# Attention over a convolved image: part sums added by accumulating transfers instead of VectorE

## The chip, the core and the metric

The kernel runs on one core of one Trainium2 chip. The metric is the device time of one execution in microseconds (us); less is better. Short names of the engines: PE is TensorE, DVE is VectorE, ACT is ScalarE, POOL is GpSimd, SP is SyncE. SP and POOL issue most of the transfers (DMAs).

## The reference

The input is four images of 384 channels and 48 x 48 points (2304 tokens). Of each image the reference computes

- `local`: a 7 x 7 convolution of each channel by itself, scaled and shifted, and a layer norm over the channels;
- `x_norm`: a layer norm of the image over the channels, and from it q, k, v by one 384 x 1152 product, in 8 heads of 48;
- `q = q + local`, `softmax(q k^T / sqrt(48)) v` for each head over all 2304 tokens, a 384 x 384 projection, and the sum of that and the image.

All of it is in 32-bit floats.

## The kernel before

**Tiling.** Channels lie on the partitions, tokens along the free axis. Two heads make a *pair*, so there are 4 pairs (`NP`). The queries of an image are worked in 5 *groups* (`NA`) of 8, 10, 10, 10 and 10 image rows, that is 384 or 480 tokens; with four images there are 20 groups, `t` = 0 to 19 (`NT`). The keys are 18 blocks of 128 (`KB`), taken in 3 batches of 6 (`BATCH`). A group therefore has 12 *slots* (`NSLOT`): slot `s` is pair `s // 3` and batch `s % 3`.

**A slot.** `score_batch` makes the scores of six key blocks on PE (L952), and ACT takes their exponentials (L960). `weigh_batch` multiplies them by the values on PE (L967) and sums over the six blocks in PSUM; the row behind the 48 of each head is the softmax's denominator, so the result of a pair stands on 64 + 49 = 113 partitions. `sums_out` then lets ACT copy it to SBUF. The first batch of a pair goes straight into the pair's place in `ao` (pairs 0 to 2) or `ao3` (pair 3, in the profile `aot`), by L859. The second and third go to a tile `part` of their own with tag `part_o` and two buffers (L849; in the profile the tile is `o`), and wait in the list `parts_of`. One `sums_add` in each slot takes the oldest of these and adds it to the pair's place (L868). After the third part it also issues, on SP, two small DMAs of the denominators to `den` in DRAM (L873), and after pair 3 six DMAs that bring rows of `ao3` to their place in `ao` (L877).

**The convolution.** Most of DVE's time goes to the convolution of the *next* group: 147 multiply-and-add instructions per group (L307), fed out of a queue `stream`. A planner (`plan`) deals them to points in the slots, from hand-estimated spare times; its numbers are fixed in the code. The next group's norm needs them done by a given slot: PE forms the mean over the channels (`mean_kept`, L568 with `mean_w`), DVE subtracts it (`centre`, L489), and so on to that group's queries (`query_end`, `high_queries`, `low_queries`). `low_queries` ends in SP DMAs that move rows inside the tile `qs` (L830, L832), and PE's scores wait for these.

**Between images** PE makes keys, values and queries of the next image in six steps (called the key stage here), and the output of the image before; DVE and ACT take their results from PSUM. Keys are written in pieces to `wide` in DRAM by POOL's DMAs (L591 to L619); in each slot one DMA (`load_keys`, L628) fetches the stack `ks` for two slots later, into one of three buffers.

**Division.** In slot 2 of the following group (or step 1 of the key stage) `divide` reads the denominators back, inverts them on DVE (L889), and spreads them by SP DMAs; in slot 7 DVE multiplies (L1259) and POOL stores the group's result (`hold`, L919).

**Order.** The instructions of PE, DVE and ACT stand in the order in which the program issues them. Those of POOL and SP are placed by a scheduler at build time, one queue each, and executed in that order: an instruction that waits holds up all behind it. POOL's DMAs also take turns on eight completion counters, so a DMA waits for an earlier one on its counter.

The first of the two places where a part is handed on:

```
        if i:
            part = work.tile([P, GM], F32, tag="part_o", name=f"o{t}_{p}_{i}")[:, :n]
            nc.scalar.copy(part[0 : 64 + HA], sums[0 : 64 + HA, 0, :n])
            parts_of.append((t, p, i, part))
            return
```

Of the kernel before, what the change touches and what calls it, by code (L numbers as in the profile page):

```python
# [13 lines left out]
ALU = mybir.AluOpType  # L14
# [33 lines left out]
def unshifted_pass(  # L48
# [16 lines left out]
    nc = tc.nc  # L65
# [10 lines left out]
    HA = HD + 1  # L76
    PAD = KS // 2
    NA = len(ROWS)
    NT = B * NA
# [121 lines left out]
    for c in range(CC):  # L201
        for r, n, first in ((0, HD, 0), (64, HD, 1), (48, 16, 6), (112, 16, 7)):
            head = first + 2 * c if first < 6 else first
            ch = head * HD + (16 * c if first >= 6 else 0)
            while n:
                part = min(n, P - ch % P)
# [654 lines left out]
    def sums_add():  # L861

        if not parts_of:
            return
        t, p, i, part = parts_of.popleft()
        ao, ao3, den = outputs[t]
        dst = (ao[:, p, :] if p < CC else ao3)[0 : 64 + HA]
        nc.vector.tensor_add(dst, dst, part[0 : 64 + HA])  # L868
        if i < KB // BATCH - 1:
            return  # L870
        for j in range(2):
            r = 64 * j
            nc.sync.dma_start(out=den[2 * p + j : 2 * p + j + 1], in_=dst[r + HD : r + HA])  # L873
        if p == NP - 1:
            for c in range(CC):
                for r in (0, 64):
                    nc.sync.dma_start(  # L877
                        out=ao[r + HD : r + 64, c, :], in_=ao3[r + 16 * c : r + 16 * c + 16]
                    )
# [231 lines left out]
    for t in range(NT):  # L1111
        b, g = divmod(t, NA)
        if g == 0 and b:

            sums_add()
            load_x(b, NG - 1)
            norms_x = {}
# [67 lines left out]
        for s in range(NSLOT):  # L1185
            pair, part = divmod(s, KB // BATCH)
# [40 lines left out]
            if early and s == first + 3:  # L1227
                low_queries(t + 1, 0)
            convolve("slot", t, s, 0)
            sums_add()  # L1230
            if early and s == first + 1:
                norm.centre()
# [39 lines left out]
            if following and s == first + 1:  # L1272
                norm.sum_squares()
                norm.out()

    sums_add()
    for i, at in enumerate(pieces_out):
        ao, n = aos[i], size(at)
# [555 lines left out]
```

## Time and profile before

| | |
|---|---|
| median of 3 runs | 2784.97 us (2781.41 to 2786.35) |
| the profiled execution: time / span of its trace | 2782.53 us / 2780.7 us |
| PE busy | 2749.9 us, 99% of the span |
| DVE busy | 2339.9 us, 84% |
| ACT busy | 1639.0 us, 59% |
| POOL busy | 696.2 us, 25% |
| mean share of the 16 DMA engines on POOL's queue / SP's queue | 35.4% / 12.2% |

The span runs from the first to the last instruction; the execution's time is 1.8 us longer. The shares of busy time are over all stages. A wait is written as the instruction that waited, and what released it. A line "L868" is that line of the kernel. In an entry such as `113x480 f32` the first number counts partitions, the second elements on each.

### The profile page before, as it was taken

What the parts mean: (1) busy time and instruction counts of PE and PEld (TensorE: products, weight loads), DVE (VectorE), ACT (ScalarE), POOL (GpSimd) and SP (SyncE); (2) the same over time, 40 slices, a digit from 0 to 9 for tenths busy, and PEclk for the clock granted to TensorE, in tenths of its full rate; (3) what the DMA queues carried; (4) which work ended last, traced back from release to release, by engine and by line L of the source; (5) the groups of instructions that cost most, each with busy time, mean ns of one, the idle gap of its engine ahead of it and who ended that gap; (6) DMA issues with size and microseconds to landing.
All of it is one profiled execution on the core that took longest, in us unless ns stands there. A gap on an engine that the chain in (4) does not pass through costs nothing.

```text
span 2780.7 us, 46399 instructions
## 1 busy us (share of the span) xinstructions
PE 2749.9 (99%) x16438; PEld 1555.9 (56%) x16438; DVE 2339.9 (84%) x4082; ACT 1639.0 (59%) x2281; POOL 696.2 (25%) x1273
## 2 busy tenths in 40 slices
PE   9998999999999999999999999999999999999999
PEld 6565555555555655555556665555555565555555
DVE  6879999989999999989888899898898889987112
ACT  4345666666423766776632566767652276676662
POOL 5731111111375111110257311101117701110110
PEclk9999999999999999999999999999999999999999
DMA  7344444445355454454545554545535545444442
GB/s 143 98 112 126 118 122 131 122 129 134 124 165 153 129 141 138 120 143 133 159 107 152 159 135 128 137 124 145 137 116 165 140 130 133 138 128 135 141 145 74
DMA packets 163298, 369.15 MB, mean 133 GB/s; under 512 B 61488, under 2 KB 112208, under 8 KB 163056
## 3 DMA queue, kind: packets, MB, share of 16 engines
q0 software_dynamic: 76992, 284.75, 35.4%
q1 hardware_dynamic: 83072, 77.72, 12.2%
q10 hardware_dynamic: 2992, 3.62, 0.4%
q8 instruction: 132, 2.16, 0.3%
q14 instruction: 110, 0.90, 0.1%
HBM read 258.14 MB, written 64.14 MB: 116 GB/s over the span
## 4 chain that ended last, share of the span: by engine, by line
PE 87%; DVE 5%; POOL 4%; DMA 2%; issue 1%; ACT 1%; SPq 0%; DVEq 0%; ACTq 0%; POOLq 0%
PE o L967 40%; PE r L952 32%; PE r L568 14%; DVE acc L307 4%; POOL wide L594 1%; DMA wide<-k 1%; DMA slab<-in_x_dram 1%; POOL wide L619 1%; POOL wide L592 1%; POOL wide L591 0%; POOL wide L613 0%; DVE k L661 0%; PE r L322 0%; DMA qs<-qs 0%; PE r L1010 0%
## 5 line engine op out<-in xcount | busy, mean ns | idle before, releaser
L307 DVE SCALAR_TENSOR_TENSOR acc<-slab,vec,acc 128x450 f32<-128x450 f32 (+8 forms) x2854 | 1679.8, 657 | 2.2
L960 ACT ACTIVATE pt<-r 128x960 f32<-128x960 f32 (+1 forms) x1440 | 1248.4, 943 | 236.4 <-PE o L967 148.9
L967 PE MATMUL o<-pt,v 128*64 128x480 f32 (+1 forms) x5760 | 1167.9, 555 | 4.1 <-ACT pt L960 4.1
L952 PE MATMUL r<-qs,ks 64*128 64x480 f32 (+1 forms) x8640 | 970.9, 374 | 9.5 <-DMA qs<-qs 6.3
L952 PEld LDWEIGHTS r<-qs,ks 64*128 64x128 f32 x8640 | 784.9, 184 | 277.6 <-issue 168.2
L967 PEld LDWEIGHTS o<-pt,v 128*64 128x64 f32 x5760 | 393.1, 137 | 663.7 <-issue 581.7
L628 POOL DMA_DIRECT2D ks<-wide x228 | 165.5, 726 | 1361.2 <-PE r L952 1328.9
L568 PE MATMUL r<-xn,w_qk 128*128 128x384 f32 x864 | 283.7, 486 | 0.0
L849 ACT COPY o<-o 113x480 f32<-113x480 f32 (+1 forms) x160 | 87.1, 544 | 299.4 <-PE o L967 299.4
L568 PEld LDWEIGHTS r<-xn,w_qk 128*128 128x128 f32 x864 | 164.2, 190 | 114.5
L868 DVE TENSOR_TENSOR ao<-ao,o 113x480 f32<-113x480 f32 (+1 forms) x120 | 76.1, 634 | 96.1 <-ACT o L849 96.0
L568 PE MATMUL r<-w_v,xn 128*128 128x384 f32 x432 | 144.8, 487 | 0.0
L650 ACT COPY v<-r 128x384 f32<-128x384 f32 x72 | 32.1, 480 | 188.3 <-PE r L568 188.3
L568 PEld LDWEIGHTS r<-w_v,xn 128*128 128x128 f32 x432 | 81.5, 190 | 58.3 <-issue 2.9
L594 POOL DMA_DIRECT2D wide<-k x192 | 96.6, 508 | 11.3 <-issue 8.3
L859 ACT COPY ao<-o 113x480 f32<-113x480 f32 (+1 forms) x60 | 32.7, 545 | 101.9 <-PE o L967 101.9
L619 POOL DMA_DIRECT2D wide<-k x192 | 92.7, 488 | 0.0
L613 POOL DMA_DIRECT2D wide<-k x144 | 72.1, 503 | 76.0 <-ACT k L658 60.4
L108 POOL DMA_DIRECT2D slab<-in_x_dram x76 | 47.1, 627 | 153.6 <-DVE acc L307 153.4
L825 DVE TENSOR_TENSOR qs<-xn,qs 128x480 fp32r<-128x480 f32 (+1 forms) x60 | 38.0, 633 | 56.2 <-ACT qs L820 56.1
L568 PE MATMUL r<-af,w_o 128*128 128x384 f32 (+1 forms) x270 | 85.2, 470 | 0.0
L675 ACT ACTIVATE xn<-r,qkb 128x384 f32<-128x384 f32 x72 | 41.0, 578 | 64.7 <-PE r L568 63.1
(139 smaller groups left out, 1348.1 us busy)
## 6 DMA issues: line engine op xcount, KB each, us to landing
ks<-wide POOLq DMA_DIRECT2D x228, 768.0 KB, 5.2
qs<-qs SPq DMA_DIRECT2D x352, 60.0 KB
wide<-k POOLq DMA_DIRECT2D x480, 24.0 KB, 1.9
slab<-in_x_dram POOLq DMA_DIRECT2D x24, 432.0 KB, 8.1
wide<-k POOLq DMA_DIRECT2D x192, 48.0 KB, 1.8
wide<-ks POOLq DMA_DIRECT2D x12, 768.0 KB, 4.4
xr<-in_x_dram POOLq DMA_DIRECT2D x16, 576.0 KB, 5.3
rb<-rden SPq DMA_DIRECT2D x32, 270.0 KB
```

The costliest lines, as they stand in the source:

```text
L108: queue.dma_start(out=dst[p0 : p0 + piece.shape[0]], in_=piece)
L307: nc.vector.scalar_tensor_tensor(dst, src, weight, dst, ALU.mult, ALU.add)
L568: nc.tensor.matmul(dst, lhsT=weights(c), rhs=src(c), start=c == 0, stop=c == CC - 1)
L594: queue.dma_start(out=dst[r + 32 * i : r + 32 * i + 32, 1], in_=k[r + 16 : r + HD, 1])
L613: nc.gpsimd.dma_start(out=last[16 * u : 16 * u + 16, 0], in_=k[r : r + 16, 0])
L619: nc.gpsimd.dma_start(out=last[to : to + 16, 1], in_=k[r : r + 16, 1])
L628: nc.gpsimd.dma_start(out=place_keys(b, p, i), in_=wide[b, p][:, :, at])
L849: nc.scalar.copy(part[0 : 64 + HA], sums[0 : 64 + HA, 0, :n])
L868: nc.vector.tensor_add(dst, dst, part[0 : 64 + HA])
L952: nc.tensor.matmul(r[:, j, :n], lhsT=ks[rows, w, at], rhs=qs[rows, m, :], start=i == 0, stop=i == 2,)
L960: nc.scalar.activation(pt, r[:, :, :n], AF.Exp, scale=SCALE)
L967: nc.tensor.matmul(sums[halves[j], 0, : columns_of(t)], lhsT=values[t // NA, kb // NB][:, first : first + 64], rhs=pt[:, j, :], start=i == ...
```

## The change

`sums_add` adds the second and the third part of a pair by a DMA on POOL's queue that reads the part and adds it to the destination in SBUF, instead of by a DVE instruction. In the last two groups the DVE instruction stays.

```
@@ -865,7 +865,10 @@
         t, p, i, part = parts_of.popleft()
         ao, ao3, den = outputs[t]
         dst = (ao[:, p, :] if p < CC else ao3)[0 : 64 + HA]
-        nc.vector.tensor_add(dst, dst, part[0 : 64 + HA])
+        if t < NT - 2:
+            nc.gpsimd.dma_start(out=dst, in_=part[0 : 64 + HA], accum_op=ALU.add)
+        else:
+            nc.vector.tensor_add(dst, dst, part[0 : 64 + HA])
         if i < KB // BATCH - 1:
             return
         for j in range(2):
```

Lines behind it move down by three (L952 becomes L955, and so on); the transfers stand at L869, the remaining instructions at L871. The order on DVE and ACT is otherwise the same. On POOL each transfer stands, by the build, between the key loads of its slots; on SP a few DMAs change places, among them, in the key stage, the read of the denominators (L888), which moves behind eight DMAs of the first key stack.

## The prediction

> **What bounds the kernel.** I read the page's busy times and chain first, then PE's waits, then the stretch where the longest of them lies, and last the transfers that are nearest to the new one.
>
> ```profile
> PE 2749.9 (99%) x16438; PEld 1555.9 (56%) x16438; DVE 2339.9 (84%) x4082; ACT 1639.0 (59%) x2281; POOL 696.2 (25%) x1273
> ...
> PE 87%; DVE 5%; POOL 4%; DMA 2%; issue 1%; ACT 1%; SPq 0%; DVEq 0%; ACTq 0%; POOLq 0%
> ...
> L868 DVE TENSOR_TENSOR ao<-ao,o 113x480 f32<-113x480 f32 (+1 forms) x120 | 76.1, 634 | 96.1 <-ACT o L849 96.0
> ```
>
> PE is the bound: 2780.7 - 2749.9 leaves it 30.8 us of idle time. The adds take DVE's time, and DVE even waits before them, but only what shortens PE's idle time can shorten the run. PE's own waits:
>
> ```profile
> PE r L568 <- DVE acc L307: 7.8, 1, 7.8
> PE r L952 <- DMA qs<-qs: 6.3, 5, 2.4
> PE o L967 <- ACT pt L960: 4.1, 3, 2.1
> PE r L952 <- ACT pt L960: 3.2, 4, 1.1
> ```
>
> (total, times, longest). Only the first waits for DVE: once, 7.8 us, for the convolution. It is in group 0, whose slots are the short ones (384 tokens). PE in order of time there (start, length, line, count, and in brackets the idle time before):
>
> ```profile
> 246.69 5.14 PE L568 MATMUL r<-acc,mean_w 128*128 128x480 f32 x6 [7.80 <-DVE acc L307]
> 251.76 3.48 PE L952 MATMUL r<-qs,ks 64*128 64x384 f32 x36
> 255.17 4.09 PE L967 MATMUL o<-pt,v 128*64 128x384 f32 x24
> 259.19 2.68 PE L568 MATMUL r<-sq,mean_w 128*128 128x480 f32 x6
> ```
>
> Six matmuls took 5.14 us after the wait, and six of the same form 2.68 us later. The table of stretches shows why (stretch, its length, busy time of PE, PEld, DVE, ACT and POOL, and then the granted clock, the DMA share and GB/s):
>
> ```profile
> 242.00:244.00 2.00, 0.00 (x0) 0.00 (x0) 1.89 (x4) 0.00 (x0) 0.00 (x0) 0.50 0.00 0
> ...
> 248.00:250.00 2.00, 2.00 (x3) 0.67 (x2) 2.00 (x4) 0.00 (x0) 1.90 (x4) 0.50 0.98 206
> ...
> 252.00:254.00 2.00, 2.00 (x24) 2.00 (x26) 2.00 (x4) 1.68 (x3) 0.00 (x0) 1.00 0.98 154
> ```
>
> In the wait the clock fell to half, and it came back only at about 252. So this place costs 7.8 us, and 2.5 us of slow matmuls.
>
> **What the change removes.** 18 groups of 8 adds: 144 of the 160. Of these 32 are in the groups of 384 tokens (rows of 0.55 us) and 112 in those of 480 (0.65 us): 32 x 0.55 + 112 x 0.65 = 90 us of DVE's 2339.9. Nearly all of it lies beside PE, which did not wait for DVE. On PE's path stand only the adds between the start of group 0's slots and the end of that convolution. DVE in order of time:
>
> ```profile
> 188.23 0.55 DVE L868 TENSOR_TENSOR ao<-ao,o 113x384 f32<-113x384 f32 x1
> 188.70 9.34 DVE L307 SCALAR_TENSOR_TENSOR acc<-slab,vec,acc 128x480 f32<-128x480 f32 x15
> 197.95 0.56 DVE L868 TENSOR_TENSOR ao<-ao,o 113x384 f32<-113x384 f32 x1
> ...
> 216.01 0.56 DVE L868 TENSOR_TENSOR ao<-ao,o 113x384 f32<-113x384 f32 x1
> ...
> 225.15 0.55 DVE L868 TENSOR_TENSOR ao<-ao,o 113x384 f32<-113x384 f32 x1
> ...
> 237.03 9.51 DVE L307 SCALAR_TENSOR_TENSOR acc<-slab,vec,acc 128x480 f32<-128x480 f32 x13
> 246.46 0.55 DVE L868 TENSOR_TENSOR ao<-ao,o 113x384 f32<-113x384 f32 x1
> ```
>
> Four adds stand before the convolution's end; the fifth begins as it ends. Each puts the next instruction back by 0.47 us (188.70 - 188.23), so the convolution ends 4 x 0.47 = 1.9 us sooner. No other work fills in, as DVE shows no wait here. The wait becomes 5.9 us; the clock had fallen after some 3 us of it, so the slow matmuls stay, and the gain is **1.9 us**, up to 2.5 if the clock returns a step sooner. What is late next is the 2.41 us wait for `qs` at 278: it hangs on ACT, on DVE's query instructions and on SP, has no add in front of it after 253, and stays. The key stages lose nothing: their waits (1.41 and 1.57 us in the first) hang on SP's queue of DMAs behind DVE's last keys, and the one add at their start (736.70, after 3.00 us of DVE waiting) is followed by other DVE waits of some 10 us in the same stage.
>
> The Trainium skill (TensorE: Matmul & The Clock Gate, Part 1) says that the clock halves after an idle window of about 3.4 us and that the window runs freely. By it a wait of 5.9 us still halves the clock, and the return can shift by a window from run to run.
>
> **What it adds on POOL.** 144 issues at 0.5 (a 48-row DMA) to 0.73 us (a key load) are 72 to 105 us on an engine that is idle for 1328.9 us before its key loads alone: hidden. Each transfer waits for ACT's copy, and the third part's also for the second part's landing, since both add to the same bytes. Behind a waiting transfer stand the next key load, slab and image loads; for its landing wait ACT's copy two parts later (two buffers), SP's `den` DMAs with the `qs` DMAs behind them, and then `divide`.
>
> **How long one takes** no row shows, since none accumulates. The nearest are:
>
> ```profile
> ks<-wide POOLq DMA_DIRECT2D x228, 768.0 KB, 5.2
> ...
> wide<-k POOLq DMA_DIRECT2D x480, 24.0 KB, 1.9
> ...
> held<-ao POOLq DMA_DIRECT2D x12, 720.0 KB, 3.8
> ```
>
> (count, KB each, us from issue to landing.) `held<-ao` moves 384 rows of 1920 B, `wide<-k` 16 rows. If both use all 16 DMA engines, they have 24 rows and 1 row on each, so a row costs (3.8 - 1.9) / 23 = 0.083 us. The new transfer has 113 rows of 1920 B: 8 on an engine, 1.9 + 7 x 0.083 = **2.5 us**; if reading the destination doubles the row, 3.1. But 113 is not a multiple of 16, as every row count above is. Should all rows go to one engine, it is 1.9 + 112 x 0.083 = 11.2 us, and doubled 20.5. I take 2.5 to 3.1: these DMAs are of the same kind on the same queue. The ends for the range are 2.5 and 20.5; below 2.5 nothing more would be gained, as the wait is not PE's.
>
> The Trainium skill (DMA: Bandwidth & Descriptors, "Why a DMA increments its semaphore by 16 and not by 1") speaks against my choice: the number of engines is the largest divisor up to 16 of the slowest dimension, which for 113 is 1, and only some direct copies on this queue are spread regardless. By it the sum would be that of the first rival below. No trace here shows such a row count.
>
> **What covers a landing.** A slot of 480 tokens is 9.08 us. After the second part's copy, POOL issues: that transfer, a key load, (9 us later) the third part's, a key load. The latter's keys are first read 4 x 9.08 = 36.3 us after the second part's PE work ends; copy 0.56 and issue 0.73 come off: 35.0 left for two landings, one after the other, and 5.2 of the load behind them: 2 x 3.1 + 5.2 = 11.4, or 9.08 + 3.1 + 5.2 = 17.4 with the slot between. Covered by far. ACT's copy needs its buffer 27 us after the transfer may start: covered. In a group's start, `den` waited for an add 4 us after ACT's copy (512.4 to 516.3); 0.7 + 3.1 is the same, so `divide` in slot 2 finds its numbers. In the key stage the read of the denominators moves from 742 behind the key stack, to about 755; DVE wants it at 765.74.
>
> **Sum.** 2782.5 - 1.9 = 2780.6 for an execution like the profiled one. The median is 2.4 above that execution, so the forecast is 2784.97 - 1.9 = **2783 us**: no change that a measurement can tell, whose bound I take at 0.2% or 5.6 us.
>
> **Rivals.**
> *One engine does all rows* (slower). The third part's transfer stands in that engine's queue before the key load's rows. It decides where 2 x L + 5.2 passes 35.0, at a landing L of 14.9 us. At 11.2 nothing is lost; at 16, 2.2 us for each of 72 pairs, 158 us; at 20.5, 11.2 x 72 = 806 us. For it: 113 rows, a read of the destination that no row here has. Against: POOL's loads of 16 and 48 rows land in about 2 us. Chance 0.20.
> *Crowding* (slower). In 210 to 220 us the DMA engines are 0.79 busy and PE already waits 0.44 us for `qs`; at 278 it waits 2.41. If a new transfer delays these two by 3.1 us each and the second wait also halves the clock (2.5 us), that is 8.7 - 1.9 = 6.8 more, 2792; with the same in the key stages' three starts, 3 x (3.1 + 2.5) = 17 more, 2809. Against: `qs` elsewhere has some 10 us to spare (issued 525.5, read from 539). Chance 0.15.
> *The wait vanishes* (faster). If DVE's convolution also ran quicker without the adds, by 5 us over the 66 us, the clock would hold, and 7.8 + 2.5 = 10.3 us would go: 2775. Against: the convolution's instructions have no wait behind an add. With the spread of 5 us between runs, chance 0.10.
> *Nothing of it reaches PE* gives 2785 and lies in the forecast, whose chance is 0.55.
>
> The forecast's own range is 2780 to 2788. For 8 in 10 the range takes in the third rival's half, all of crowding, and the foot of the first: 2777 to 2835; the rest of the one-engine case, about 0.15, is left out, and 0.03 below.
>
> **What would show it.** Right: no L868 adds before group 18, the wait at 246 near 5.9 us, the new transfers landing in 2.5 to 4 us, no new PE wait. Wrong: PE or ACT waiting for `ks`, or ACT's `o` copies waiting for a DMA; landings over 15 us; POOL's key loads released by a DMA and not by PE; or PE's waits at `qs` grown to several us.

## The result, and the profile after

The changed kernel takes **2795.22 us** (median of 7 runs, 2791.45 to 2798.54) where the kernel before takes 2784.97: ratio 1.0036, 95% interval 1.0026 to 1.0046. The forecast was 2783 us and no change that can be measured; it is 10 us slower, beyond the 5.6 us taken as the bound. The profiled execution took 2795.22 us, its span 2793.4 us against 2780.7, that is 12.7 us more.

The page's busy times, the chain, and the costliest groups' line of the new transfers (busy us, mean ns; idle time of POOL before them):

```profile
PE 2754.3 (99%) x16438; PEld 1561.1 (56%) x16438; DVE 2258.9 (81%) x3938; ACT 1638.7 (59%) x2281; POOL 828.9 (30%) x1417
...
PE 85%; DMA 5%; DVE 4%; POOL 3%; issue 2%; ACT 1%; SPq 0%; DVEq 0%; ACTq 0%; POOLq 0%
...
L869 POOL DMA_DIRECT2D ao<-o x108 | 97.9, 907 | 378.4 <-ACT o L849 303.2
```

DVE lost 81 us of work and POOL gained 133 us. PE is still the bound; its idle time went from 30.8 to 39.1 us and its busy time up by 4.4 us, though it executes the same matmuls. PE's waits (total, times, longest) say where the idle time came from:

```profile
PE r L955 <- DMA qs<-qs: 16.3, 10, 5.4
PE r L568 <- DVE acc L307: 6.0, 1, 6.0
PE o L970 <- ACT pt L963: 3.9, 3, 2.1
PE r L955 <- ACT pt L963: 3.2, 4, 1.0
```

The wait for the convolution shrank by 1.8 us, as forecast. The wait for `qs` grew by 10.0 us, from five places to ten. With the 4.4 us of slower matmuls that is 10.0 + 4.4 - 1.8 = 12.6 of the 12.7 us. In PE's timeline (start, length, line, count; idle time before and its end in brackets) the first line is the place in group 0, and the other four are waits that were not there before:

```profile
245.91 5.14 PE L568 MATMUL r<-acc,mean_w 128*128 128x480 f32 x6 [5.96 <-DVE acc L307]
...
996.57 4.17 PE L955 MATMUL r<-qs,ks 64*128 64x480 f32 x35 [1.26 <-DMA qs<-qs]
...
1110.87 6.39 PE L955 MATMUL r<-qs,ks 64*128 64x480 f32 x36 [5.37 <-DMA qs<-qs]
...
1673.78 3.69 PE L955 MATMUL r<-qs,ks 64*128 64x480 f32 x31 [0.55 <-DMA qs<-qs]
...
2030.52 5.08 PE L955 MATMUL r<-qs,ks 64*128 64x480 f32 x31 [2.35 <-DMA qs<-qs]
```

The longest shows the mechanism. ACT copied the part of pair 3 to `o`, and was done at 1078.90:

```profile
1078.34 0.56 ACT L849 COPY o<-o 113x480 f32<-113x480 f32 x1 [2.13 <-PE o L970]
```

POOL then did this:

```profile
1089.04 1.15 POOL L108 DMA_DIRECT2D slab<-in_x_dram  x1 [14.68 <-DVE acc L307]
1090.18 0.94 POOL L869 DMA_DIRECT2D aot<-o  x1
1090.76 1.52 POOL L108 DMA_DIRECT2D slab<-in_x_dram  x2
```

and SP this:

```profile
1095.08 0.50 SPq L876 DMA_DIRECT2D den<-aot  x2
1095.63 3.80 SPq L880 DMA_DIRECT2D ao<-aot  x6
1101.78 0.35 SPq L891 DMA_DIRECT2D rd<-den  x1
1102.23 0.51 SPq L832 DMA_DIRECT2D qs<-qs  x1
...
1105.68 1.32 SPq L832 DMA_DIRECT2D qs<-qs  x2
```

The first and the last of these in the kernel before:

```profile
1082.87 0.51 SPq L873 DMA_DIRECT2D den<-aot  x2
...
1093.15 1.34 SPq L832 DMA_DIRECT2D qs<-qs  x2
```

The transfer was ready to go at 1078.90 and was issued at 1090.18, 11.3 us later: ahead of it on POOL stood the image load of the next convolution (`load_slab`, L108), which waited 14.68 us until DVE's convolution let go of the buffer. SP's `den` DMAs came at 1095.08 instead of 1082.87 in the kernel before, and the last `qs` DMA, behind them on SP, was issued by 1107.0 instead of 1094.5. (Some 1.4 us of these 12 us are an earlier lag of the whole run: PE's scores of the slot before began at 1096.36 and 1095.00.) PE was ready for that pair at 1105.5 and waited 5.37 us. The table of stretches (PE busy, then the other engines; granted clock, DMA share, GB/s at the end) shows the second half of the price:

```profile
1106.00:1108.00 2.00, 0.00 (x0) 0.00 (x0) 0.00 (x0) 0.10 (x1) 0.00 (x0) 1.00 0.96 190
1108.00:1110.00 2.00, 0.00 (x0) 0.00 (x0) 0.00 (x0) 0.00 (x0) 0.88 (x1) 0.62 0.39 86
1110.00:1112.00 2.00, 1.13 (x5) 1.06 (x7) 1.89 (x6) 0.00 (x0) 0.00 (x0) 0.50 0.85 113
...
1114.00:1116.00 2.00, 2.00 (x14) 1.82 (x14) 2.00 (x4) 1.71 (x2) 0.00 (x0) 0.67 1.05 211
1116.00:1118.00 2.00, 2.00 (x15) 1.09 (x13) 1.90 (x5) 1.09 (x2) 0.45 (x1) 1.00 0.82 129
```

The clock fell to half in the wait and stayed there until about 1115, so the 36 score matmuls took 6.39 us where 4.15 were enough at 1096.

The wait of 1.26 us at 997 came in the same way: 8.3 us on POOL's queue, from the end of ACT's copy (968.21) to the issue (976.48). The other two new waits are of a second kind. Before the one of 2.35 us at 2030, POOL and SP did this:

```profile
2002.84 0.71 POOL L108 DMA_DIRECT2D slab<-in_x_dram  x1 [10.03 <-DVE acc L307]
2003.54 0.73 POOL L628 DMA_DIRECT2D ks<-wide  x1
2004.27 0.94 POOL L869 DMA_DIRECT2D ao<-o  x1
```

```profile
2014.99 0.52 SPq L876 DMA_DIRECT2D den<-ao  x2
```

The part was copied by 2000.69, so the queue held the transfer for only 3.6 us; but it took 10.7 us to land, where the median of all transfers is 4.0 (3.5 to 12.1), and SP's `den` DMAs, with `qs` behind them, waited for that. For the wait of 0.55 us at 1674 it was 4.4 us of queue and a landing of 11.6 us, from 1642.70 to 1654.3. The third part's transfer adds to the same bytes and had to wait for it: its part was copied by 1645.71, and it was issued at 1654.91. Both slow transfers were issued right behind DMAs of the image load and a key load of 768 KB; the transfer at 1090.18, with a single DMA of the image load just ahead of it, landed in 4.9 us. So a place behind the image load can cost twice, on POOL and in the landing. That the loads just ahead make the landing long is read from these three places and not tested by itself.

### The profile page after: what moved, and what is told of

It reads as the page before. It is cut to its first block, busy times and chain, and to the rows that moved or that the text cites. A ratio compares the mean times of both kernels' runs of the same rounds, so it can differ in the third digit from the quotient of the medians.

```text
span 2793.4 us, 46587 instructions
## 1 busy us (share of the span) xinstructions
PE 2754.3 (99%) x16438; PEld 1561.1 (56%) x16438; DVE 2258.9 (81%) x3938; ACT 1638.7 (59%) x2281; POOL 828.9 (30%) x1417
## 3 DMA queue, kind: packets, MB, share of 16 engines
q1 hardware_dynamic: 83072, 77.72, 12.1%
## 4 chain that ended last, share of the span: by engine, by line
PE 85%; DMA 5%; DVE 4%; POOL 3%; issue 2%; ACT 1%; SPq 0%; DVEq 0%; ACTq 0%; POOLq 0%
PE o L970 38%; PE r L955 31%; PE r L568 15%; DVE acc L307 2%; DMA qs<-qs 2%; DMA aot<-o 1%; DMA wide<-k 1%; DMA slab<-in_x_dram 1%; DMA ao<-aot 1%; POOL wide L594 1%; PE r L322 1%; POOL wide L619 1%; POOL wide L592 0%; POOL wide L591 0%; POOL wide L613 0%
## 5 line engine op out<-in xcount | busy, mean ns | idle before, releaser
L955 PE MATMUL r<-qs,ks 64*128 64x480 f32 (+1 forms) x8640 | 976.2, 375 | 19.4 <-DMA qs<-qs 16.3
L955 PEld LDWEIGHTS r<-qs,ks 64*128 64x128 f32 x8640 | 790.1, 185 | 287.7 <-issue 179.7
L628 POOL DMA_DIRECT2D ks<-wide x228 | 171.9, 754 | 759.0 <-PE r L955 659.5
L869 POOL DMA_DIRECT2D ao<-o x108 | 97.9, 907 | 378.4 <-ACT o L849 303.2
L825 DVE TENSOR_TENSOR qs<-xn,qs 128x480 fp32r<-128x480 f32 (+1 forms) x60 | 38.0, 633 | 98.2 <-ACT qs L820 98.1
L108 POOL DMA_DIRECT2D slab<-in_x_dram x76 | 51.9, 732 | 142.0 <-DVE acc L307 140.9
L460 DVE TENSOR_TENSOR sq<-sq 128x384 f32<-128x384 f32 (+1 forms) x33 | 19.5, 591 | 78.0 <-ACT sq L455 78.0
```

The lines of the kernel that those rows point to most:

```text
L108: queue.dma_start(out=dst[p0 : p0 + piece.shape[0]], in_=piece)
L628: nc.gpsimd.dma_start(out=place_keys(b, p, i), in_=wide[b, p][:, :, at])
L869: nc.gpsimd.dma_start(out=dst, in_=part[0 : 64 + HA], accum_op=ALU.add)
L955: nc.tensor.matmul(r[:, j, :n], lhsT=ks[rows, w, at], rhs=qs[rows, m, :], start=i == 0, stop=i == 2,)
```

## The experiments

Two theories stood at the start. **Q**, the queue: a transfer that stands behind a waiting image load on POOL starts some 10 us late, and its lateness goes through SP's queue to `qs` and PE. **C**, crowding: the transfers load the DMA engines, and everything on them, the `qs` DMAs among it, lands later. "Before" below is 2784.15 to 2784.80 us, run beside each set.

**Only pairs 0 to 2.** SP's chain of `den`, `ao<-aot` and `rd` hangs on pair 3, so the first pair of experiments splits the transfers there: 108 of the 144, then the other 36.

```
-        if t < NT - 2:
+        if t < NT - 2 and p < NP - 1:
```

> 108 transfers stay (pairs 0 to 2); the 36 sums of pair 3, behind which the denominators' DMAs of the whole group stand, go back to VectorE. Theory Q (queue): the loss comes from the transfers of pair 3 that stand on POOL's queue behind a slab load which waits for VectorE's convolution; SP's denominator and row DMAs wait for them, and the qs DMAs behind these come late. Then the PE waits at 997 (1.3 us), 1111 (5.4) and 1674 (0.6) vanish with their half clock, the one at 2030 (2.4, a pair below 3) may stay: ratio 1.000 to 1.001, 2784 to 2787 us. Theory C (crowding): the loss comes from the transfers' load on the DMA engines: three quarters of it stay, ratio 1.0027, about 2792 us.

Measured: 2785.17 us, ratio 1.0006 [0.9997, 1.0015]. Three quarters of the transfers cost nothing that can be measured. Of the four new waits one is left (2.51 us, at 2024), and one of 1.89 us is new at 1352. Both are of the second kind: these transfers were issued at 1997.58 and 1325.39 among the DMAs of an image load, and `den` followed 10.6 and 11.2 us later.

**Only pair 3.**

```
-        if t < NT - 2:
+        if t < NT - 2 and p == NP - 1:
```

> The reverse: only the 36 sums of pair 3 (18 groups) go by transfer, the 108 of pairs 0 to 2 by VectorE. Theory Q: the waits after group changes stay, ratio 1.002 to 1.004, 2790 to 2796 us. Theory C: a quarter of the load, ratio 1.001, about 2787 us.

Measured: 2800.38 us, ratio 1.0059 [1.0045, 1.0072]. A quarter of the transfers costs more than all of them, 4 us above the expected range. PE's longest wait for `qs` lies at the same place:

```profile
1118.80 6.43 PE L955 MATMUL r<-qs,ks 64*128 64x480 f32 x36 [4.80 <-DMA qs<-qs]
```

Its span is 6.1 us longer than that of the changed kernel. In three places PE waits 5.8 us more: the wait in group 0 (7.95 instead of 5.96, the VectorE adds are back there), the wait for `qs` in group 0 behind it (4.14 instead of 2.42), and the first scores of the second image (three waits of 2.77, 0.59 and 0.33 instead of one of 1.55). Elsewhere it waits less: its idle time grew by 4.1 us in all (43.2 instead of 39.1) and its busy time by 2.0. Why the latter two places grew was not followed up.

**All transfers, ahead of the image load.** POOL's queue is ordered at build time. Here the image load of the next group is told to stand behind the last transfer recorded, and the line that records the transfer moves ahead of the convolution's in the slot. The number of transfers and what they move stay.

```
     def conv_ops(t):
         if t + 1 < NT:
-            load_slab(*divmod(t + 1, NA))
+            with tc.issue_after(transfers[-1].ins) if transfers else ExitStack():
+                load_slab(*divmod(t + 1, NA))
...
-            convolve("slot", t, s, 0)
             sums_add()
+            convolve("slot", t, s, 0)
```

> All 144 transfers, but each sum is handed on ahead of the slot's convolution, and each slab load is queued on POOL behind the latest transfer, so that (but for one place in the third image) no ready transfer stands behind a slab load. Theory Q: the new PE waits vanish, ratio 0.999 to 1.001, 2782 to 2787 us. Theory C: the same bytes at nearly the same times, ratio 1.003 to 1.004, 2793 to 2797 us.

Measured: **2781.99 us**, ratio 0.9991 [0.9982, 1.0000]. The whole loss is gone. POOL's timeline of the same stretch, and PE's waits:

```profile
1080.23 0.86 POOL L873 DMA_DIRECT2D aot<-o  x1 [4.84 <-ACT o L852]
1089.82 2.27 POOL L108 DMA_DIRECT2D slab<-in_x_dram  x3 [8.72 <-DVE acc L310]
```

```profile
PE r L960 <- DMA qs<-qs: 7.3, 6, 2.5
PE r L571 <- DVE acc L310: 6.9, 1, 6.9
```

The transfer goes at 1080, right after ACT's copy, and the load, behind it, goes at 1089.82, where it went at 1089.72 in the kernel before. Crowding as the cause of the loss is refuted: 144 transfers with the same bytes on the same engines, and the wait for `qs` is 7.3 us where 6.3 was before. Single transfers still land late (3.5 to 12.3 us, median 3.9), but PE's six waits for `qs` all lie in group 0 and at the starts of images.

**Copy instead of accumulate**, at the same places. The kernel then leaves out the sums: the place of a pair holds only the last part.

```
-            nc.gpsimd.dma_start(out=dst, in_=part[0 : 64 + HA], accum_op=ALU.add)
+            nc.gpsimd.dma_start(out=dst, in_=part[0 : 64 + HA])
```

> The transfers copy the part over the sum and don't add it (the output lacks the other parts); order and waits are the same. What the addition costs by itself: landing 2.5 us (worked out from the plain rows) against 3.5 to 4.6. Theory Q: the transfers still stand behind the slab loads, ratio 1.002 to 1.0035. Theory C: the load of the added bytes halves or better, ratio below 1.0015.

Measured: 2792.32 us, ratio 1.0031 [1.0022, 1.0041]. The loss needs no accumulation; a plain copy at the same place in the queue costs nearly the same (7.9 us, where the changed kernel loses 10.3). What accumulating costs on the DMA engines is seen in the DMA issues (count, KB each, median us from issue to landing), first the changed kernel, then this one:

```profile
ao<-o POOLq DMA_DIRECT2D x84, 211.9 KB, 4.6
aot<-o POOLq DMA_DIRECT2D x28, 211.9 KB, 3.8
```

```profile
ao<-o POOLq DMA_DIRECT2D x84, 211.9 KB, 3.6
aot<-o POOLq DMA_DIRECT2D x28, 211.9 KB, 2.7
```

About 1 us more to land, and 0.91 instead of 0.56 us to issue on POOL.

**The denominators' DMAs behind `qs` on SP.** This cuts the way over SP inside an image, and leaves the transfers as late as they are.

```
+        late.append((t, p, dst))
+        if not (p == NP - 1 and t < NT - 2 and t % NA < NA - 1):
+            denominators()              # the den and ao<-aot DMAs
...
-                low_queries(t, pair + 1)
+                denominators(low_queries(t, pair + 1))   # issued after the last qs DMA
```

> All 144 transfers as in the changed kernel, behind the slab loads too; but within an image the DMAs that need pair 3's sums on SP (two den, six ao<-aot, and the read of the denominators behind them) stand behind the six qs DMAs of the next pair, not ahead of them. Theory Q (the late transfer reaches PE through SP's queue, where qs stands behind den): PE's waits at qs fall from 16.3 us to some 6, the two new ones of 1110 and 2030 are gone, and the time is 2782 to 2786. DVE still waits 40 us or more at the denominators, since the transfers are as late as before. Rival D (it reaches PE through DVE, whose reciprocal waits up to 15.7 us with the work of later slots behind it): the reciprocal comes even later, so the time stays at 2795 or goes above.

Measured: 2821.10 us, ratio 1.0134 [1.0118, 1.0149]: a miss, on the side of rival D. The trace holds both. The waits near 996, 1111 and 1673 are gone, as theory Q says. The one near 2030 is gone too, but not by this edit, which leaves the `den` DMAs of pairs 0 to 2 ahead of `qs`: in this run the transfer there was issued before the image load (2020.90 and 2029.67). The denominators are read later, though, and DVE's reciprocal, in order ahead of the later slots' work, now waits 133 us in 16 places instead of 46.5 us in 6:

```profile
DVE rd L909 <- DMA rd<-den: 133.1, 16, 16.4
```

```profile
1126.82 0.34 DVE L909 RECIPROCAL rd<-rd 128x30 f32<-128x30 f32 x1 [16.39 <-DMA rd<-den]
...
1147.03 0.65 DVE L825 TENSOR_TENSOR qs<-xn,qs 128x480 fp32r<-128x480 f32 x1
```

```profile
1154.98 1.17 PE L972 MATMUL r<-qs,ks 64*128 64x480 f32 x4 [4.29 <-DMA qs<-qs]
```

The query instruction of the pair after (L825) came so late that PE waited for that pair's `qs` instead. So a late transfer has two ways to PE: over SP, and over DVE. The edit closed one and widened the other.

**Transfers in group 0 alone**, the prediction's gain by itself (`if t == 0:`).

> Transfers in group 0 alone (8 of 144), VectorE adds everywhere else. The prediction's own gain by itself: the convolution's end comes 4 x 0.47 = 1.9 us sooner, so PE's wait for it is near 6 us instead of 7.8. Time 2782 to 2784, ratio 0.9990 to 0.9997, which lies at the edge of what a measurement can tell. Crowding of the DMA engines in group 0 would show as longer waits at qs (0.44 and 2.41 us before) and take the gain back: 2785 or more.

Measured: 2783.48 us, ratio 0.9997 [0.9988, 1.0006]; the wait is 6.90 us and the six matmuls behind it 4.60 us. The point estimate lies 1.3 us under before, and the interval cannot tell it from none.

**The moved line alone**, in the kernel before: the VectorE add of a slot ahead of the slot's first convolution instructions.

```
-            convolve("slot", t, s, 0)
             sums_add()
+            convolve("slot", t, s, 0)
```

> The kernel before, with the VectorE add of a slot moved ahead of the slot's first convolution instructions; no transfers. It shows what the moved line alone does. Theory Q: nothing, 2784 to 2786, ratio 0.9995 to 1.0005, so that the transfers ahead of the slab loads with their 2782 owe nothing to the moved line. Rival O (the time came back through the order on DVE): 2781 to 2783, ratio 0.9985 to 0.9993.

Measured: 2788.81 us, ratio 1.0016 [1.0007, 1.0025]. Neither was expected: the line costs 4 us. DVE's adds to `ao` now wait 156.2 us for ACT's copy instead of 96.0, and PE's wait in group 0 is 10.3 us instead of 7.8. Rival O, that the time came back through this line, falls all the more.

**The changed kernel with the moved line** and without the ordered image load.

> The changed kernel with the same line moved and no other edit: the scheduler then still puts several of pair 3's transfers behind a slab load that waits. Theory Q: PE waits at qs for 12 to 17 us in all, 2791 to 2796, ratio 1.002 to 1.004. Rival O: 2781 to 2783 as with the transfers ahead of the slab loads.

Measured: 2797.00 us, ratio 1.0044 [1.0030, 1.0058], PE's wait for `qs` 15.6 us; the time is 1 us above the expected range, the wait within it. POOL's order is again that of the changed kernel:

```profile
1090.21 1.14 POOL L108 DMA_DIRECT2D slab<-in_x_dram  x1 [14.46 <-DVE acc L307]
1091.35 0.94 POOL L869 DMA_DIRECT2D aot<-o  x1
```

This kernel and the one of 2781.99 us differ in one thing, whether the image load or the transfer stands first on POOL. That is worth 15 us, more than the whole loss.

**Which of the two ways the changed kernel took.** The division moved two slots later, so that DVE no longer waits for the denominators; SP's order stays.

```
-            if s == 2 and g:
+            if s == 4 and g:
                 rb = divide(t - 1)
```

> The changed kernel with the division two slots later and no other edit: the way over DVE is cut, the way over SP stays, as den, ao<-aot and the read of the denominators still stand ahead of the qs DMAs. Theory Q2: in the changed kernel all new waits of PE came over SP, so DVE's wait at the denominators falls from 46.5 us to under 10, PE's waits at qs stay at 13 to 18, and the time stays at 2792 to 2797. Rival D (it came over DVE after all): 2781 to 2786 and qs waits of 6 to 8 us.

Measured: 2809.77 us, ratio 1.0097 [1.0082, 1.0113]. DVE's wait for the denominators fell from 46.5 to 1.9 us, and the two long waits of PE stayed where they were:

```profile
997.46 4.16 PE L955 MATMUL r<-qs,ks 64*128 64x480 f32 x35 [1.30 <-DMA qs<-qs]
...
1110.58 6.98 PE L955 MATMUL r<-qs,ks 64*128 64x480 f32 x36 [4.21 <-DMA qs<-qs]
```

So these did not come over DVE: theory Q2 holds on the place, together with the experiment above on SP's order, in which they went. It fails on the time, which is 15 us above the changed kernel, and on PE's waits for `qs`, 21.5 us in all; the control accounts for 9.8 of the 15.

**The later division in the kernel before.**

> The kernel before with the division in slot 4 alone. A control: DVE waited there for 4.1 us in all and PE not at all, so 2784 to 2786, ratio 0.9995 to 1.0005. If it were 2781 or less, the gain of the versions with the later division would owe nothing to the transfers.

Measured: 2793.92 us, ratio 1.0043 [1.0027, 1.0058]: the supposed neutral move costs 9.8 us without any transfer. The division's own SP DMAs now stand ahead of the `qs` DMAs of pair 2, and PE waits there:

```profile
1247.46 3.71 PE L952 MATMUL r<-qs,ks 64*128 64x480 f32 x31 [1.36 <-DMA qs<-qs]
1360.09 3.70 PE L952 MATMUL r<-qs,ks 64*128 64x480 f32 x31 [2.17 <-DMA qs<-qs]
```

**Both ways cut**, and transfers still behind the image loads.

> The version with the denominators' DMAs behind the next pair's qs DMAs on SP (it gave 2821), and besides the division two slots later (slot 4 instead of 2). Transfers still stand behind waiting slab loads on POOL. Theory Q2 (a late transfer reaches PE by two ways and no other: SP's queue, den ahead of qs; and DVE's queue, reciprocal ahead of the work behind it): with both cut, DVE's wait at the denominators falls from 133 us to under 15, PE's waits at qs from 24.0 to 6 to 8, and the time is 2781 to 2785. Rival C (the transfers' load on the DMA engines): the qs DMAs still land late; 2790 or more. Rival P (the slab load's delay itself, by key loads behind it on POOL): PE waits for ks, 2790 or more.

Measured: 2803.56 us, ratio 1.0074 [1.0060, 1.0088]; the expected 2781 to 2785 was missed. The waits near 997 and 1111 are gone and DVE's wait for the denominators is 4.6 us, but PE waits 20.6 us in all for `qs`, with new ones at 1135, 1248, 1363, 1925 and 2037. Those at 1248, 1363 and 1925 are in the control too. The later division costs 9.8 us by itself, so this run doesn't say what the queue on POOL costs once both ways are cut; that stays open.

**All three edits together.**

> All three edits: transfers ahead of the slab loads, denominators' DMAs behind the qs DMAs, division in slot 4. If the queues held everything that was lost, there is nothing left to win over the transfers ahead of the slab loads alone (2782): 2780 to 2783, ratio 0.9985 to 0.9993, PE's waits at qs 6 to 8 us. A time of 2777 or less would show a cost that is still hidden.

Measured: 2784.36 us, ratio 1.0004 [0.9995, 1.0013], 1.4 us over the expected range, with waits for `qs` at 1243 and 1354 again. So the three together win nothing over the transfers ahead of the image load alone. As the later division brings waits of its own, this doesn't show that nothing is left to win. The version with the transfers ahead of the image load, at 2781.99 us, is the best of all, 2.5 us below before beside which it ran, at the edge of what can be told from no change; its interval ends at 1.0000.

## Why the prediction was wrong

**The step that failed: "Each transfer waits for ACT's copy, and the third part's also for the second part's landing".** The prediction named what stands *behind* a waiting transfer on POOL (key loads, slab and image loads) and the chain that waits for its landing ("SP's `den` DMAs with the `qs` DMAs behind them, and then `divide`"). It did not ask what a transfer stands behind. So "In a group's start ... 0.7 + 3.1 is the same" put the time from ACT's copy to the landing at 3.8 us. At 1078.90 it was 11.3 us of queue and then 4.9 to `den`, 16.2 together, where the kernel before had 5.3 (1077.53 to 1082.87): 10.8 us more. The prediction gave `qs` "some 10 us to spare (issued 525.5, read from 539)", but left out its landing. At this place the kernel before had 9.6 us from the last issue to the scores (1094.5 to 1104.06); with the 3.9 us to the scores that the changed kernel shows (1107.0 to 1110.87), an estimate, 5.7 were spare, and 10.8 - 5.7 = 5.1 is near the wait of 5.37. The text ahead of the prediction has each transfer "between the key loads of its slots"; what it leaves out is that an image load can stand there too, as at 1089.04. The length of such a wait was to be read in the trace of before, in POOL's waits, a view that the prediction used for key loads alone:

```profile
POOL ks L628 <- PE r L952: 1328.9, 187, 12.2
POOL slab L108 <- DVE acc L307: 153.4, 15, 18.3
```

Fifteen waits, up to 18.3 us, in which everything behind them on POOL stands still. POOL's mean load, 25 to 30%, says nothing of that.

**The gain was about right.** DVE's busy time fell by 81 us where 90 was forecast (the rows of 0.55 and 0.65 us overlap the next instruction; the path's own 0.47 allowed for that), and the wait in group 0 went from 7.80 to 5.96 us where 5.9 was forecast; the slow matmuls after it took the same 5.14 us. In the runs with transfers in all of group 0, wait and matmuls together took 10.9 to 12.0 us (6.70 + 4.21 to 6.89 + 5.14) against 12.94 before, a gain of 0.9 to 2.0.

**The landing was undersized**, a median of 3.5 to 4.6 us by size and place for 2.5 to 3.1, and the issue on POOL 0.91 us for 0.5 to 0.73. One number for all landings was the larger fault: the longest took 12.1 us, and landings of 10.7 and 11.6 us made two of the four new waits, 2.9 of 9.5 us. With the order changed, medians of 3.5 to 4.2 us cost nothing.

**Rival "one engine does all rows": refuted.** The queues' packets, bytes and share of 16 engines, before and after:

```profile
q0 software_dynamic: 76992, 284.75, 35.4%
```

```profile
q0 software_dynamic: 97728, 314.63, 44.2%
```

20736 packets more are 144 for each transfer, 9 on each of 16 engines if they lie evenly. With the queue's other packets taken as unchanged, 8.8% of 16 x 2793.4 us over 144 is some 27 us of engine time per transfer (good to some 3 us, as kernels without transfers have 35.4 to 36.1% for the same packets), which cannot pass in 4.6 us on fewer than six engines. The Trainium skill (DMA: Bandwidth & Descriptors, "Why a DMA increments its semaphore by 16 and not by 1") gives one engine for 113 rows and excepts some direct copies on this queue; the trace agrees with the exception, not with the rule.

**Rival "crowding": right number, another cause in the main.** It gave 2792 to 2809 us by late `qs` and a halved clock, and late `qs` and a halved clock are what came. But it let the DMA engines delay `qs`, in group 0 and the key stages. Those waits changed little (0.44 to 0.54 us, 2.41 to 2.42, 1.41 to 1.55), the new ones lie elsewhere, and the experiment with all transfers in a better order refutes the transfers' load as their cause. What comes near to it is the slow landing at two of them, but there it is the transfer that lands late, behind the loads, and not `qs`.

**Rival "the wait vanishes"** did not happen: 5.96 us of wait are left, in the best version 6.89.

## What to carry to other kernels

Before work moves to a queue that executes in order, list what each new entry will stand *behind*, and how long that waits in the old trace, not only what will stand behind it: a queue that is 25% busy can still be shut for 18 us at a time. Then order the queue so that short work on which others wait goes ahead of long-range loads; here one such order was worth 15 us and turned a loss into none. A control for each edit of an experiment is worth its run: two moves that looked free cost 4 and 10 us by themselves.

## What the runs showed of the hardware

An accumulating transfer within SBUF, 113 rows of 1920 bytes, costs the DMA engines nearly twice what the same copy does: some 27 us of engine time against 15 (4.8% of 16 x 2792.8 us over 144), each good to some 3 us; that is some 0.24 us a row (27 us over 113). It lands 1 us later in the median.

The granted clock of PE fell in shorter waits than expected. At 2030 PE waited 2.35 us and the clock of the next stretch was 0.52:

```profile
2028.00:2030.00 2.00, 0.17 (x1) 0.00 (x0) 2.00 (x4) 0.00 (x0) 0.00 (x0) 1.00 1.19 214
2030.00:2032.00 2.00, 1.48 (x8) 1.39 (x10) 2.00 (x4) 0.64 (x1) 0.00 (x0) 0.52 0.90 236
```

31 matmuls took 5.08 us where 3.69 were enough after a wait of 0.55 us. The Trainium skill (TensorE: Matmul & The Clock Gate, Part 1) has an idle window of about 3.4 us; here 2.35 us of idle time sufficed. A wait of this length does not always do it: after 2.42 us near 280 the clock stayed at 1.00 in the changed kernel, and 35 matmuls took 4.17 us; after 2.42 us at the same place in the kernel with the transfers ahead of the image load it fell to 0.50, and they took 5.74 us.
